# Set-up by halves of the images, in a four-layer convolution kernel on one Trainium2 core

## Chip, cores and metric

The kernel runs on one core of a Trainium2 chip. Its time is the device time of one execution in microseconds (us). Five engines with instruction queues of their own take part: TensorE (PE, with its weight loads PEld), VectorE (DVE), ScalarE (ACT), GpSimd (POOL) and SyncE (SP), which here only issues DMAs.

## Reference

Four layers, each adding a function of the group-normalised input to the input. The change lies wholly in the start of layer 0, whose function is a matrix in tensor-train form with three cores.

```python
def _gn(v, G=8, eps=1e-5):
    B_, H_, W_, C_ = v.shape
    g = v.reshape(B_, H_, W_, G, C_ // G)
    m = jnp.mean(g, axis=(1, 2, 4), keepdims=True)
    s = jnp.var(g, axis=(1, 2, 4), keepdims=True)
    return ((g - m) / jnp.sqrt(s + eps)).reshape(v.shape)
...
# x: (1024, 16, 16, 16) float32
x = x + _L0_conv_ref(_gn(x), L0_conv_core0, L0_conv_core1, L0_conv_core2)
x = x + _L1_conv_ref(_gn(x), ...)
x = x + _L2_conv_ref(_gn(x), L2_conv_filters, L2_conv_bias)
x = x + _L3_conv_ref(_gn(x), ...)
```

The normalisation of layer 0 needs, for every image and each of 8 groups of 2 channels, the mean and the variance over the whole image: no value of an image can be normalised before the whole image has been read.

## The kernel before

**Layer 0.** The 1024 images are two blocks of 512 (the constant NB). The layer's 4096x4096 matrix is cut into blocks, and the block products are taken by a table of fast-multiplication terms (OUTER, 13 entries, and inside each INNER, 7 entries). One entry of OUTER is a *phase*; it has four *units* (q = 0 to 3); a unit has seven *products*, named in INNER: s2, s5, w11, s1, s7, w01, w00. Each product is done in two *halves* (`go(0)` and `go(1)` in `pieces`, L1565), so a phase is 56 halves. A half is four matmul calls of 128x128 weights on 128x256 data (L1586); a call leaves two records in the profile, so a half is eight records.

**What a unit needs.** `build(u, h)` (L1466) makes the weights w00, w01 (h = 0) or w10, w11 (h = 1) of unit u: 16 small matmuls of `gq`, which comes from the tensor-train cores, with `R` into four PSUM banks (L1478), then four copies by ACT (L1483). `mix` (L1508, L1510) adds or subtracts two such weights on DVE: s2, s5, s1, s7, w01. `gather` (L1616) adds a product from PSUM into the unit's result `r`, on ACT for the first use of a quarter and on DVE later.

**The data of phase 0.** Its images are the first 512. A phase's data has four blocks (b, n): b is the half of the image's columns, n is the half of the images (n = 0 is images 0 to 255, n = 1 is 256 to 511). Of INNER, s2 multiplies block (0,0), w11 block (1,0) (after (0,0) has been taken off it), s5 block (1,1), w00 block (0,1); s1, s7 and w01 multiply the sums E0, E1, E2 that `combined` (L1220) makes of several blocks on DVE.

**The set-up, in order of the program** (L2059 to L2110). SP loads the first 512 images as eight transfers of 1 MB (L1091), all of them at once. `stats` makes one BN_STATS per image group, channel group and half image on DVE, 64 in all (L1103); `aggregate` joins them (L1133); `root`, `newton` and `widen` turn them into mean and 1/deviation (L1136 to L1151); `spread` transposes these (L1159, copied by ACT at L1160). `turn` (L1105) transposes the images: four transposes into one bank, then a copy by ACT; there are 32 turns, 16 of them (`lines[0]`) ahead of the first product and 16 (`lines[1]`) woven into phase 0. Only then `first_normed` subtracts the mean and multiplies (L1191) block by block.

Meanwhile `early` (L663) makes the g of units 0 and 1, and `keep_g` (L649) stores it into DRAM with 12 transfers on POOL; `gload` (L1439) reads it back as `gq`. Twelve later pieces of g (`piece`, L680) are made between the halves of phase 0.

**Order.** Every engine runs its instructions in the order in which the program states them; there is no scheduler. `before` (L2090) is a table: the half of phase 0 with that number is preceded by these steps. `run` (L2006) spreads further lists over the halves of a phase between two fractions; `part_steps(1)` makes the data of phase 1 on DVE, between 0.43 and 0.99 of phase 0.

Of the kernel before, what the change touches and what calls it, by code (L numbers as in the profile page):

```python
# [21 lines left out]
P = 128  # L22
# [83 lines left out]
def conv_preact_kernel(ctx: ExitStack, tc: tile.TileContext, a: dict, out: bass.AP):  # L106
# [484 lines left out]
    def train_setup(room):  # L591
# [71 lines left out]
        def early():  # L663

            g = work([P, 2, 8, P], "w0", "gw")
            pg = [bank([P, 2, 4, 64], "w", "pg") for _ in range(4)]
            for x in range(2):
                for k in range(4):
                    for r in range(4):
                        gmul(pg[r][:, x, k], 0, k % 2, x, r, k // 2)  # L670
            for q, x, r in product(range(2), range(2), range(4)):
                f = 64 * x + 16 * r
                A.copy(
                    g.rearrange("p q (o i) f -> p q i o f", i=2)[:, q, :, :, f : f + S],
                    pg[r][:, x, 2 * q : 2 * q + 2].rearrange("p i (o j) -> p i o j", j=S),
                )
                if (x, r) == (1, 3):
                    keep_g(0, q, g[:, q].rearrange("p (o i) f -> p o (i f)", i=2), G)
# [399 lines left out]
    def input_steps(n, tag, queue):  # L1078
# [4 lines left out]
        slots = flats[1 - n].rearrange("p (s f) -> p s f", s=8)  # L1083
        X = part_lines(0)

        def slot(half, bg):
            return slots[:, 0 if (n, half, bg) == (1, 1, 3) else 4 * half + bg]

        def load(half, bg):
            b0 = n * NB + bg * P  # L1090
            queue.dma_start(  # L1091
                slot(half, bg),
                a["x"][b0 : b0 + P, 8 * half : 8 * half + 8].rearrange("b h w c -> b (h w c)"),
            )
# [10 lines left out]
        def turn(h, wh):  # L1105
            pt = bank([P, 4, P], tag[h % len(tag)], "ptin")
            for bg in range(4):
                x = slot(h // 8, bg).rearrange("p (h w f) -> p h w f", h=8, w=2)
                T.transpose(pt[:, bg], x[:, h % 8, wh], ident)
            pt = pt.rearrange("p g b -> p (g b)")  # L1110
            if n == 0 and h < 8:
                if wh:
                    A.copy(X[:, 1, h], pt)
                else:
                    A.copy(raw[:, h], pt.rearrange("p (n i) -> p n i", n=2))
                return
            if h % 2 == 0:
                st["l"] = work([P, 2, NB], "t4", "lines")
            A.copy(st["l"][:, h % 2], pt)
            if h % 2 == 1:  # L1120
                nc.sync.dma_start(
                    xr[n][wh, h - 1 : h + 1].rearrange("h p b -> p h b"), st["l"]
                )
# [32 lines left out]
        def spread(k):  # L1156
            pt = bank([P, 4, P], tag[0], "ptmr")
            for bg in range(4):
                T.transpose(pt[:, bg], st["e", k][:, bg], ident)  # L1159
            A.copy(mr[n][:, k], pt.rearrange("p g b -> p (g b)"))  # L1160

        def kept(b):
            to = xr[n][b, 0:8]
            if b:
                G.dma_start(to.rearrange("h p b -> p h b"), X[:, 1])
                return
            for i in range(2):
                G.dma_start(
                    to.rearrange("h p (n b) -> p h n b", n=2)[:, :, i], raw[:, :, i]
                )  # L1170
# [15 lines left out]
        return loads, stat, lines, tail, [lambda: spread(0), lambda: spread(1)], kept  # L1186
# [6 lines left out]
    def first_normed(b, i):  # L1193

        X, E = part_tile(0)
        cols = slice(256 * i, 256 * i + 256)

        def op(t, k):
            x = X[:, b, t : t + 4, i]
            centre_scale(x, x if b else raw[:, t : t + 4, i], 0, cols, k)  # L1200

        return [(1.2, lambda t=t, k=k: op(t, k)) for t in (0, 4) for k in range(2)]
# [201 lines left out]
    def layer_train():  # L1404
# [60 lines left out]

        def build(u, h):  # L1466

            if u >= len(units):
                return
            R, gs = st["R", units[u][0]], list(st["g", u, h].values())  # L1470
            w = st["w", u, h] = work([P, 2, 2, 4, P], "w1" if h else "w0", "w")
            pw = [bank([P, 2, 2, P], "w", "pw") for _ in range(4)]
            for v in range(2):
                for i in range(2):
                    for k, g in enumerate(gs):
                        for r in range(4):
                            rows = slice(32 * r, 32 * r + 32)
                            T.matmul(  # L1478
                                pw[r][:, v, i], g[rows, P * (2 * v + i) : P * (2 * v + i) + P], R[rows, k],
                                start=k == 0, stop=k == len(gs) - 1,  # L1480
                            )
            for r in range(4):
                A.copy(  # L1483
                    w.rearrange("p b s t m -> p (b s t) m")[:, :, 32 * r : 32 * r + 32].rearrange(
                        "p k (v o) -> p v k o", v=2
                    ),
                    pw[r].rearrange("p v i (k o) -> p v (i k) o", o=S),
                )
# [4 lines left out]
        def mix(u, what):  # L1493

            if u >= len(units):
                return
            x, y, f, out = dict(
                s2=((1, 0), (1, 1), ALU.add, "s2"),
                s5=((0, 0), (0, 1), ALU.add, "s5"),
                s1=((1, 1), (0, 0), ALU.add, "s2"),  # L1500
                s7=((0, 1), (1, 1), ALU.subtract, "s5"),
                w01=((1, 0), (0, 0), ALU.subtract, None),
            )[what]
            into = block(u, 0, 1)
            x, y = block(u, *x), block(u, *y)
            if out:
                t = st[what, u] = work([P, 2, 4, P], out, what)
                V.tensor_tensor(t.rearrange("p s t m -> p (s t m)"), x, y, f)  # L1508
            else:
                V.tensor_tensor(into, x, y, f)  # L1510
# [7 lines left out]
        begun = set()  # L1518
# [46 lines left out]
        def pieces(u, k):  # L1565

            ph, q = units[u]
            what, where, goes = INNER[k]

            def go(i):  # L1570
                X, E = part_tile(ph)
                if i == 0:
                    at = {1: (1, 6144), 3: (1, 14336)}.get(u)
# [9 lines left out]
                po, at = st["po"], 2 * k + i  # L1583
# [3 lines left out]
                if at == 1 and u > 0:  # L1587
                    store(u - 1)
                if at == 2:
                    mix(u, "s1")  # L1590
                if at == 4:
                    mix(u, "s7")
                if at == 5:
# [5 lines left out]
                if at == 9:  # L1599
# [3 lines left out]
                if at == 12:  # L1603
# [5 lines left out]
                if i == 1:  # L1609
                    gather(u, k, po, goes)  # L1610
# [5 lines left out]
        def gather(u, k, po, goes):  # L1616
            r = st["r", u].rearrange("p s a (n i) -> p s (a n) i", n=2)
            at = {x: 2 * x[0] + x[1] for x in goes}
            if k in (2, 3, 6):
# [4 lines left out]
            for x, sign in goes.items():  # L1624
                out = r[:, :, at[x]]
                if all(x not in INNER[j][2] for j in range(k)):
# [6 lines left out]

        steps = [
            [x for u in range(4 * ph, 4 * ph + 4) for k in range(7) for x in pieces(u, k)]
            for ph in range(NP)
        ]
        return (coefs, gload, build, mix), steps
# [420 lines left out]
    with ExitStack() as es:  # L2059
        stage(es, dict(t4=4, s=2, n=2, w1=1, w0=2, s2=1, s5=1, r=1, gq=2, R=2, A=1), dict(w=4, m=1, o=3))  # L2060
        sums, cores, early, rest, sum_steps = train_setup(flats[0][:, 8192:9216])
        tag = ["w"]
        loads, stat, lines, tail, (spread0, spread1), kept = input_steps(0, tag, nc.sync)
        now(loads)

        A.activation(work([P, NB], "n", "warm")[:, 0:1], ident[:, 0:1], AF.Sqrt)
        (coefs, gload, build, mix), phases = layer_train()
        now([sums])
        coefs(0)
        now([cores] + stat[0])  # L2070
        early()
        gload(0, 1, queue=G)
        gload(0, 0, queue=G)
        now(lines[0])
        kept(0)
        kept(1)
        gload(1, 0)
        gload(1, 1)
        build(0, 1)
        build(0, 0)  # L2080
        now(stat[1] + tail[:2])
        mix(0, "s2")
        now([spread0] + tail[2:] + [spread1])
        x00, x11, x10, x01 = (first_normed(*at) for at in ((0, 0), (1, 1), (1, 0), (0, 1)))
        now(x00[0::2] + x00[1::2])
        mix(0, "s5")
        now(x11[:2])
        tag[0] = "m"
        more = combined(0)
        before = {  # L2090
            1: x11[2:] + rest[0][0:1],
            2: x10 + rest[0][1:2] + more[0:2],
            4: more[2:4],
            5: more[4:6],
            7: x01,
            8: more[6:8],
            9: more[8:10],
        }
        free = (12, 15, 18, 22, 26, 29, 32, 36, 40, 43)
        for i, piece in zip(free, rest[0][2:] + rest[1]):  # L2100
# [13 lines left out]
        for j in late:  # L2114
            sums_late(j)
        run(
            steps_of(phases[0]), 107, (), (lines[1], 0.12, 0.42), (part_steps(1), 0.43, 0.99),
        )
        tag.append("w")
        loads, stat, lines, tail, more, _ = input_steps(1, tag, G)  # L2120
# [4 lines left out]
        for i in range(4):  # L2125
            woven_in += [stat[1][i], stat[2][i]] + lines[1][4 * i : 4 * i + 4]
        run(
            steps_of(phases[1]), 107, (), ([(0, x) for x in loads[:7]] + [8] + woven_in + tail, 0.0, 0.76),
# [92 lines left out]
```

## Time and profile before

| | us |
|---|---|
| three runs of the kernel before | 2737.14 median (2736.14 to 2738.66) |
| the profiled execution | 2737.21 |
| its span in the profile | 2734.2 (so 3.0 lie outside the span) |
| PE busy | 2668.0 (98% of the span) |
| DVE busy | 1994.9 (73%) |
| ACT busy | 1241.6 (45%) |
| POOL busy | 542.9 (20%) |

Busy time by stretch of the first 260 us, from the windows of the trace (PEclk is the granted clock of TensorE, 1.00 at full):

| stretch, us | PE busy | DVE busy | ACT busy | PEclk |
|---|---|---|---|---|
| 0 to 30 | 16.4 | 25.9 | 14.4 | 1.00, 1.00, 0.95 |
| 30 to 40 | 5.64 | 5.79 | 2.70 | 0.50 |
| 40 to 50 | 5.26 | 8.27 | 2.59 | 0.50 |
| 50 to 60 | 10.00 | 9.86 | 2.58 | 0.69 |
| 60 to 70 | 10.00 | 10.00 | 3.73 | 1.00 |
| 70 to 80 | 8.50 | 9.93 | 4.07 | 1.00 |
| 80 to 130 | 49.7 | 23.1 | 18.3 | 1.00 |
| 130 to 180 | 50.0 | 45.9 | 14.6 | 1.00 |
| 180 to 190 | 7.24 | 9.96 | 0.00 | 0.83 |
| 190 to 260 | 69.0 | 56.5 | 28.7 | 1.00 |

A line of the timeline reads: start, time from the first start to the last end, engine, line of the kernel, operation, result and sources, shape, number of records, and in brackets the idle time before it with what ended it. The first half of a product begins at 46.93 us; from there on PE is busy almost without a break to the end of the kernel.

### The profile page before, as it was taken

Reading aid. Unit: us, or ns where it says so; the run is one execution under the profiler, and the core shown is the slowest. Engines: PE = TensorE matmul, PEld = TensorE weight load, DVE = VectorE, ACT = ScalarE, POOL = GpSimd, SP = SyncE. Lnnn points to the kernel's source line nnn. Section 1 sums busy time; section 2 is a strip of 40 time slices with the busy share of each in tenths; the row PEclk is TensorE's granted clock in tenths of the full one; section 3 lists DMA queues with packets and bytes.
Section 4 is the critical chain, followed back from the end, with each engine's and each line's share of the span. In section 5 each row is a group of like instructions: output and inputs, shape, how many; then the busy total and the mean of one; then the engine's idle time right before and its main releaser. Section 6 shows DMA issues by size and latency. Waiting matters only on the chain.

```text
span 2734.2 us, 47225 instructions
## 1 busy us (share of the span) xinstructions
PE 2668.0 (98%) x18990; PEld 1749.5 (64%) x18990; DVE 1994.9 (73%) x2414; ACT 1241.6 (45%) x2091; POOL 542.9 (20%) x702
## 2 busy tenths in 40 slices
PE   6999999999999999999999999999999999999997
PEld 5888888888888888888878733433333333334344
DVE  8597667867788776667888677668779858756654
ACT  3324222222232222323322366676767757676664
POOL 2001351312122632311321111111113211110000
PEclk8999999999999999999999999999999999999998
DMA  6687788998797887888689664455576865444665
GB/s 255 214 317 271 228 173 220 240 202 199 188 250 182 156 216 186 205 237 250 178 188 259 138 170 101 107 161 121 107 195 84 202 155 139 99 89 118 179 176 209
DMA packets 265945, 503.19 MB, mean 184 GB/s; under 512 B 34404, under 2 KB 102040, under 8 KB 256448
## 3 DMA queue, kind: packets, MB, share of 16 engines
q1 hardware_dynamic: 179600, 336.68, 36.9%
q0 software_dynamic: 85936, 163.37, 34.0%
q8 instruction: 150, 2.46, 0.4%
q14 instruction: 67, 0.55, 0.1%
q10 hardware_dynamic: 192, 0.13, 0.0%
HBM read 281.71 MB, written 226.49 MB: 186 GB/s over the span
## 4 chain that ended last, share of the span: by engine, by line
PE 84%; DVE 7%; DMA 5%; issue 2%; ACT 1%; SPq 1%; POOL 0%; DVEq 0%; POOLq 0%; ACTq 0%
PE po L1586 40%; PE ph L1993 21%; PE po L1822 8%; PE po L1677 5%; PE pw L1478 4%; DMA xn<-in_x_dram 1%; DVE xn L1191 1%; PE po L1686 1%; DMA xn<-xr 1%; DMA g_sum<-g_dram 1%; DMA xn<-xf 1%; PE ptx L1886 1%; DVE xn L1220 1%; DMA xb<-xn 0%; PE pcnt L1862 0%
## 5 line engine op out<-in xcount | busy, mean ns | idle before, releaser
L1996 ACT ACTIVATE hid<-ph,pack 128x512 f32<-128x512 f32 (+1 forms) x1040 | 641.4, 684 | 313.5 <-PE ph L1993 254.6
L1586 PE MATMUL po<-xn,s 128*128 128x256 f32 x3328 | 756.0, 384 | 10.1 <-DVE s L1508 7.4
L1586 PEld LDWEIGHTS po<-xn,s 128*128 128x128 f32 x3328 | 628.5, 191 | 113.1 <-issue 16.1
L1586 PE MATMUL po<-xn,w 128*128 128x256 f32 x2496 | 565.2, 382 | 1.5 <-DVE xn L1220 1.5
L1993 PE MATMUL ph<-xn,wq 32*128 32x512 f32 (+1 forms) x3752 | 518.3, 590 | 1.9 <-DVE u L1834 1.5
L1586 PEld LDWEIGHTS po<-xn,w 128*128 128x128 f32 x2496 | 468.1, 190 | 74.6 <-issue 5.9
L1483 ACT COPY w<-pw 128x512 f32<-128x512 f32 x416 | 213.6, 599 | 455.6 <-PE pw L1478 379.9
L1993 PEld LDWEIGHTS ph<-xn,wq 32*128 32x128 f32 x3752 | 233.6, 184 | 228.9 <-issue 210.0
L1993 PE MATMUL ph<-xn,pack 32*128 32x512 f32 x1288 | 274.2, 607 | 5.6 <-DVE u L1834 1.6
L1508 DVE TENSOR_TENSOR s<-w 128x1024 f32<-128x1024 f32 x208 | 251.3, 1218 | 29.0 <-PE po L1586 25.9
L1822 PE MATMUL po<-hid,pack 128*32 128x512 f32 (+1 forms) x2080 | 256.0, 592 | 0.8 <-ACT hid L1996 0.5
L1834 DVE SCALAR_TENSOR_TENSOR u<-po,pack,xn 128x512 f32<-128x512 f32 (+1 forms) x130 | 96.3, 741 | 168.1 <-PE po L1822 167.0
L1876 POOL DMA_DIRECT2D xf<-u x96 | 82.6, 861 | 618.7 <-DVE u L1874 591.0
L771 DVE TENSOR_TENSOR xn<-xn,m 128x1024 f32<-128x1024 f32 x128 | 150.2, 1217 | 34.7 <-ACT m L794 34.6
L1993 PEld LDWEIGHTS ph<-xn,pack 32*128 32x128 f32 x1288 | 115.6, 184 | 90.8 <-issue 63.2
L1822 PEld LDWEIGHTS po<-hid,pack 128*32 128x32 f32 x2080 | 53.9, 109 | 174.9 <-ACT hid L1996 86.3
L1677 PE MATMUL po<-xn,convw 128*128 128x512 f32 x368 | 163.6, 598 | 0.0
L1220 DVE TENSOR_TENSOR xn<-xn 128x1024 f32<-128x1024 f32 x130 | 152.6, 1215 | 0.0
L1478 PE MATMUL pw<-R,gq 32*128 32x128 f32 x3328 | 139.4, 286 | 7.9 <-DVE small L1133 7.3
L1622 DVE TENSOR_TENSOR r<-r,po 128x1024 f32<-128x1024 f32 x78 | 95.0, 1218 | 70.5 <-PE po L1586 57.5
L1478 PEld LDWEIGHTS pw<-R,gq 32*128 32x128 f32 x3328 | 113.9, 188 | 42.2 <-issue 38.6
L1560 POOL DMA_DIRECT2D xf<-xn x69 | 88.6, 1733 | 254.2 <-DVE xn L1553 72.3
(230 smaller groups left out, 2764.7 us busy)
## 6 DMA issues: line engine op xcount, KB each, us to landing
xn<-xf SPq DMA_DIRECT2D x128, 512.0 KB
xn<-xb SPq DMA_DIRECT2D x36, 1024.0 KB
wq<-L_conv_wy SPq DMA_DIRECT2D x192, 192.0 KB
xf<-xn POOLq DMA_DIRECT2D x69, 512.0 KB, 9.7
piece<-xb SPq DMA_DIRECT2D x64, 512.0 KB
xf<-r POOLq DMA_DIRECT2D x48, 512.0 KB, 11.7
xf<-u POOLq DMA_DIRECT2D x96, 256.0 KB, 4.1
gq<-g_dram SPq DMA_DIRECT2D x86, 256.0 KB
```

The source lines that it names most:

```text
L771: V.tensor_tensor(part, part, m().unsqueeze(1).broadcast_to([P, 2, NB]), op)
L1220: V.tensor_tensor(out, y, z, f)
L1478: T.matmul(pw[r][:, v, i], g[rows, P * (2 * v + i) : P * (2 * v + i) + P], R[rows, k], start=k == 0, stop=k == len(gs) - 1,)
L1483: A.copy(w.rearrange("p b s t m -> p (b s t) m")[:, :, 32 * r : 32 * r + 32].rearrange("p k (v o) -> p v k o", v=2), pw[r].rearrange("p v ...
L1508: V.tensor_tensor(t.rearrange("p s t m -> p (s t m)"), x, y, f)
L1586: T.matmul(po[:, i], matrix(u, what)[:, i, t], x, start=t == 0, stop=t == 3)
L1622: V.tensor_tensor(part, part, po.unsqueeze(2).broadcast_to([P, 2, 2, 256]), ALU.add)
L1677: T.matmul(st["po", h][wh], conv["fw"][:, y], X[:, 16 * wh + h + y - 1], start=y == max(0, 1 - h), stop=y == min(2, S - h),)
L1822: T.matmul(po[32 * j : 32 * j + 32], nca["w1"][:, v], hid[j], start=v == 0, stop=v == 1)
L1834: V.scalar_tensor_tensor(u, po, nca["b1"], X[:, 8 * q + w2, cols(hf)], ALU.add, ALU.add)
L1993: T.matmul(ph, w, x, start=k == 0, stop=k == len(tiles) - 1)
L1996: A.activation(h, ph, AF.Relu, bias=nca["bt"][:, r : r + 1])
```

## The change

The set-up is divided by images. The loads of images 0 to 255 come first (both halves of each image). Their statistics, mean and deviation are finished by themselves (`first_images`, with `root`, `newton`, `widen` and `spread` taking the half i), and only the turns that they need stand ahead of the first product: 8 of 32. A turn now takes two lines of 256 images instead of one of 512.

The g of units 0 and 1 goes from the tile `gw` straight to the tiles that `build` reads, with 32 transfers of 32 rows by 256 values (32 KB), 16 on SP and 16 on POOL. Behind them on SP follow the four loads of images 256 to 511, and then the stores of g to DRAM, which POOL had.

The order of the products of units 0 and 1 is s2 of unit 0, s2 of unit 1, w11 of unit 0, w11 of unit 1 (four products that use images 0 to 255 alone), then the other five of unit 0 and of unit 1. The two w11 results stay in PSUM until `catch_up` gathers them. The statistics of the rest stand on DVE among these halves, and 20 turns, the two remaining builds and the second `spread` stand on PE before half 8; the last four turns stand before halves 12 and 14. `part_steps(1)` begins at 0.3 of phase 0. In phase 1 an empty stretch of the plan becomes 11 instead of 8.

```diff
-        def early():
+        def early(to, after):
...
+            for q in range(2):
...
+                for o, t, h in product(range(4), range(2), (1, 0)):
+                    (nc.sync if h else G).dma_start(
+                        to[q, h][32 * o : 32 * o + 32, 256 * t : 256 * t + 256],
+                        gs[q][64 * h + t : 64 * h + 64 : 2, o],
+                    )
+            after()
+            for q in range(2):
+                keep_g(0, q, gs[q], nc.sync)
...
+        def turn(half, i, wh, h):
+            tag.append(tag.pop(0))
+            pt = bank([P, 2, 2, P], tag[0], "ptin")
+            for l, g in product(range(2), range(2)):
+                x = slot(half, 2 * i + g).rearrange("p (h w f) -> p h w f", h=8, w=2)
+                T.transpose(pt[:, l, g], x[:, h + l, wh], ident)
...
+            order, late = ((0, 2, 1, 3, 4, 5, 6), 2) if u < 2 else (range(7), 0)
...
+                if i == 1 and at == 3 and late:
+                    behind.append(lambda: gather(u, po, goes, made))
...
+            if ph == 0:
+                us = [(0, 0), (1, 0), (0, 2), (1, 2)] + [x for x in us if x[0] > 1 or x[1] not in (0, 2)]
...
-        loads, stat, lines, tail, (spread0, spread1), kept = input_steps(0, tag, nc.sync)
-        now(loads)
+        for bg in range(2):
+            load(0, bg)
+            load(1, bg)
...
+        now([cores, sums])
+        stats(0, 0)
         coefs(0)
-        now([cores] + stat[0])
-        early()
-        gload(0, 1, queue=G)
-        gload(0, 0, queue=G)
-        now(lines[0])
-        kept(0)
-        kept(1)
-        gload(1, 0)
-        gload(1, 1)
-        build(0, 1)
-        build(0, 0)
-        now(stat[1] + tail[:2])
-        mix(0, "s2")
...
+        stats(1, 0)
+
+        early(early_g(), lambda: now([lambda bg=bg, h=h: load(h, bg) for bg in (2, 3) for h in range(2)]))
+        stats(0, 1)
+        stats(1, 1)
+        aggregate(0)
+        aggregate(1)
+        now(turns(0, 0, 0))
+        root(0)
+        widen(0, 0)
+        newton(0)
+        widen(1, 0)
+        spread(0, 0)
+        part = turns(0, 0, 1)
+        now(part[:2])
+        spread(1, 0)
+        build(0, 1)
+        now(part[2:])
+        build(1, 1)
...
+        now(x00[0::2] + x00[1::2])
+        mix(0, "s2")
+        now(x10[0::2] + x10[1::2])
+        mix(1, "s2")
+        now(more[0:2])
...
         before = {
-            1: x11[2:] + rest[0][0:1],
-            2: x10 + rest[0][1:2] + more[0:2],
-            4: more[2:4],
-            5: more[4:6],
-            7: x01,
-            8: more[6:8],
-            9: more[8:10],
+            2: [lambda: stats(0, 2), lambda: stats(1, 2), lambda: stats(0, 3), lambda: build(0, 0)],
+            4: [lambda: mix(0, "s5"), lambda: stats(1, 3), lambda: aggregate(2), lambda: aggregate(3)]
+            + late1[:2],
+            5: [lambda: keep(1, 0), lambda: keep(0, 0)],
+            6: late1[2:] + [lambda: keep(1, 1)] + late0[:2],
+            8: late0[2:] + [lambda: build(1, 0), lambda: keep(0, 1)] + half1[0][:4]
+            + [lambda: root(1), lambda: widen(0, 1), lambda: newton(1)]
+            + half1[0][4:] + [lambda: spread(0, 1), lambda: widen(1, 1)]
+            + half1[1][:2] + [lambda: spread(1, 1)]
+            + x11[0::2] + x11[1::2] + half1[1][2:4],
+            9: [catch_up] + more[2:6],
+            10: rest[:1],
+            11: rest[1:2] + x01[0::2] + x01[1::2],
+            12: half1[1][4:6],
+            13: more[6:10],
+            14: rest[2:3] + half1[1][6:],
+            16: rest[3:4],
         }
...
-        run(
-            steps_of(phases[0]), 107, (), (lines[1], 0.12, 0.42), (part_steps(1), 0.43, 0.99),
-        )
+        run(steps_of(phases[0]), 107, (), (part_steps(1), 0.3, 0.99))
...
-            steps_of(phases[1]), 107, (), ([(0, x) for x in loads[:7]] + [8] + woven_in + tail, 0.0, 0.76),
+            steps_of(phases[1]), 107, (), ([(0, x) for x in loads[:7]] + [11] + woven_in + tail, 0.0, 0.76),
```

## Prediction

> **What bounds the kernel now.** I read the page's busy slices first: PE has 9 tenths or more in all slices but the first and the last, so time can come only from what stands ahead of the first product or from holes in PE later. Then the timeline of the first 70 us:
>
> ```profile
> PE   6999999999999999999999999999999999999997
> ...
> 30.64 2.71 DVE L1103 BATCH_NORM_STATS2 bn<-xn 128x6 f32<-128x256 f32 x8
> ...
> 33.47 2.09 PE L1478 MATMUL pw<-R,gq 32*128 32x128 f32 x32 [7.26 <-DVE small L1133]
> ...
> 41.56 0.35 DVE L1141 RECIPROCAL small<-small 128x32 f32<-128x32 f32 x1 [2.70 <-ACT small L1137]
> ...
> 43.39 4.62 DVE L1191 TENSOR_TENSOR xn<-xn 128x1024 f32<-128x1024 f32 x4
> ...
> 46.93 3.78 PE L1586 MATMUL po<-xn,s 128*128 128x256 f32 x8 [2.63 <-DVE xn L1191]
> ...
> 57.30 3.72 PE L1586 MATMUL po<-xn,s 128*128 128x256 f32 x16
> ```
>
> The last of eight image loads lets the last statistics begin at 30.64. The first build waits 7.26 us; DVE is named, but POOL's read of g out of DRAM, issued at 29.44, is the likelier releaser (such reads land 4.8 us after issue). The first half-product starts at 46.93 and takes 3.78 us; from 57.30 two take 3.72. The windows show why: the granted clock is 0.50 from 28.9 to 56.2 us.
>
> The third view is PE at the end of phase 0, with three windows of DVE:
>
> ```profile
> 175.58 7.17 PE L1586 MATMUL po<-xn,w 128*128 128x256 f32 x32
> 185.51 8.83 PE L1586 MATMUL po<-xn,s 128*128 128x256 f32 x32 [2.76 <-DVE s L1508]
> ```
> ```profile
> 90.00:100.00 10.00, 10.00 (x66) 8.71 (x65) 2.45 (x2) 5.21 (x15) 0.00 (x0) 1.00 0.89 285
> 100.00:110.00 10.00, 9.70 (x89) 8.00 (x88) 3.58 (x3) 4.72 (x11) 0.00 (x0) 1.00 0.57 207
> ...
> 170.00:180.00 10.00, 10.00 (x75) 8.54 (x74) 10.00 (x10) 2.05 (x4) 0.00 (x0) 1.00 0.96 318
> ```
>
> PE ends phase 0 at 182.75, waits 2.76 us for DVE, and does four halves in 8.83 instead of 7.17 at a clock of 0.50. DVE (third of the busy columns) is idle three quarters of the time around 95 us and full at 175: its work for phase 1 starts late.
>
> **The change, step by step.** Durations are this trace's: a statistic 0.34 (2.71/8), a DVE operation on 1024 columns 1.14 from one start to the next, a half 1.73 to 1.8 (3.78 at half clock), a build 1.1 on PE (2.1) and 2.05 on ACT, a turn 0.44 on PE (0.86) and 0.50 to 0.59 on ACT.
>
> *Ahead of the first product.* Statistics may start at about 7.7 (an estimate: before, they began unwaited at 8.81, behind `coefs`, now second). 32 at 0.34, `coefs` 0.8 and 16 aggregations at 0.087 end at 20.8; four 1 MB loads at the 410 GB/s of the windows are in by 15. Root, newton and widen, on half the columns, take 2.1 (before 41.27 to 43.47): 22.9. Block (0,0), four operations: 27.5. On PE, g takes 3.7 us from about 10, its 16 ACT copies 2.8, to 16.5; turns and spreads follow, build (0,1) runs at 23.9 to 26.0 on PE and to 28.05 on ACT; s2 is ready at 29.2. Two turns and build (1,1) stand ahead of half 0 and need banks that ACT still reads, to 30.9. First half at **31**, 16 us earlier.
>
> *The moves of g.* No row shows one 32 KB tile-to-tile transfer. The nearest are the small weight loads: L607 on SP, four in 2.22 us, L614 on POOL, four in 2.25 and landed 2.2 later. So eight take 4.5 to issue, and those of build (0,1), from 15.2, are in by 22: under the cover of the statistics. [...] The rows show issues 0.56 apart with several under way, so I take the rows. Bounds: 0 and 3 us.
>
> *SP's queue.* It had nothing between 8.1 and 35.7 us; now it has 16 moves, four loads (issued from 23, in at about 34; DVE wants them from 37), 12 stores of g (0.65 to 0.75 each to issue), and four stores of turned images. The line stores behind them free the buffers of turns: 6 MB at 300 to 400 GB/s need 15 to 20 us from 34, and the last waits for its turn to near 56 anyway, so I count nothing. POOL has 16 moves in place of its stores and reads; at 0.56 each they are in by 27, ahead of build (0,0).
>
> *Halves 0 to 7.* I take the clock as cold for halves 0 and 1: 31 to 38.6. Build (0,0) to 40, halves 2 and 3 to 43.5, two turns, halves 4 and 5 to 47.9, four turns at ACT's pace, halves 6 and 7 to 53.8. DVE alongside: block (1,0), s2 of unit 1, the subtraction to 37.3, 24 statistics, s5, eight more, aggregation to 50.7. It then needs a square root that stands on ACT behind six turns and build (1,0).
>
> *The new wait.* Behind half 7 ACT has two copies, the build's 2.05, eight copies, root and spread: 1.1 + 2.05 + 4.4 + 0.7 = 8.2. So DVE starts on block (1,1) at **62**, after idling some 10 us. Queued behind are all sums, and PE's half 8.
>
> *From 62 to half 18.* DVE, from its start on (1,1): block 4.6, s1 5.7, two gathers of 0.6 to 6.9, E0 to 9.2, E1 to 11.5, gather, s7 to 13.3, w01, block (0,1) to 19.0, gather 20.2, E2 to 22.5. PE follows: half 8 at 3.5, halves 10, 11 at 8.1 and 10.9, 12 at 13.5, 14 at 21.3 (after a hole of 2.3), 18 at 29.4. So half 18 stands at 91.4. Before, it stood at 97.76, and 85.0 us later phase 0 was done. That stretch had five turns (2.4) that are now done, and one piece of g less (1.04): 83.6, to 175.0 instead of 182.75: **7.75 us**.
>
> *The boundary.* From half 18 to phase 1, DVE has some 56 operations of 1.14, seven of 0.6 and `coefs`: 68 us in 83.6, because its part begins at 0.3 instead of 0.43. So the hole of 2.76 goes and with it the cold halves behind it (8.83 - 7.17 = 1.66): **4.4 us**. Next late there is the load of phase 1's data, wanted 5 us after it lands. The 11 in phase 1 moves statistics that PE doesn't wait for (0 to 1 us either way; I take 0).
>
> *The sum.* 7.75 + 4.4 = 12.1 us off the profiled execution's 2737.21 (span 2734.2 and 3.0 outside it), which stands within 0.1 of the median of the runs: **2725**.
>
> [...] Here the clock came back 3.4 us after it fell behind the hole at 185, but only at 56.2 after work that began at 46.93, 9.3 us. PE works nearly without break from 21.7 on in the new order. [...] By the row it is 2725; I take the row, since it is the same place of the kernel. [...]
>
> **Rivals.**
> 1. *The boundary stays.* DVE is full to the end as before, since its steps wait for loads and stores that now queue on SP. For it: two DMA waits of 1.93 and 0.62 us in that stretch before. Against: 15 us of slack. Only 7.75 is won: 2729.5.
> 2. *The lead is hidden.* All products beyond the four need images 256 to 511, which are normalised later than before (62 against 49), so a longer wait there eats the lead. If line buffers, loads or ACT's order cost another 8 us, block (1,1) starts at 70: 2733.
> 3. *Slower: the clock.* PE's work is cut by waits and stays at half clock through halves 0 to 7 and their turns. Then, from 31: eight halves 30.2, build 2.1, six turns 5.2: 68.5; the block behind half 7, now PE's, 11.9: block (1,1) at 80.4, 18.4 late, less 12.1: 6.3 slower, 2743.5. It decides once block (1,1) starts after 74. For it: 27 us at 0.50 before. Against: from half 0 to half 7 PE hardly idles, and continuous work always brought the clock back within 9.3 us.
> 4. *It doesn't do what it says:* half 0 still waits for all loads. The order of instructions excludes that: its waits are on the first four.
>
> **Chances and range.** Forecast 0.45 (2722 to 2728), with the warm clock 0.15 more (2718 to 2722), rival 1 0.14, rival 2 0.15, rival 3 0.10; rest 0.01. Three executions lie within 0.1%; 0.2% (5.5 us) is what can be told from no change, so faster means below 2731.7. That takes the forecast, the warm case, rival 1 and a little of rival 2: 0.77; rival 2's rest and a milder rival 3: 0.13; slower 0.10. The range runs from the warm case with a cheap block (DVE could start it at 53.3 at best) to rival 2: 2716 to 2736.
>
> **What would show it.** First half near 31; DVE idle for about 10 us ahead of a start on block (1,1) near 62, ended by ACT; a hole of some 2 us ahead of half 14 at full clock; half 18 near 91; phase 1 starting near 175 with no hole and a clock of 1.00. A wait of build (0,1) for the moves beyond 24, a clock of 0.50 beyond 40, or a hole at phase 1 would make it wrong.

## The result and the profile after

| | before | changed |
|---|---|---|
| median of the runs, us | 2737.39 (2736.14 to 2738.66, 4 runs) | 2724.81 (2722.89 to 2727.75, 4 runs) |
| ratio to before | | 0.9954, 95% interval 0.9942 to 0.9966 |
| profiled execution, us | 2737.21 | 2722.89 |
| its span, us | 2734.2 | 2720.6 |
| PE busy, us | 2668.0 | 2662.2 |
| DVE busy, us | 1994.9 | 1994.4 |

The changed kernel is faster by 12.6 us in the medians; 12.1 was forecast. The work is nearly the same (DVE's busy time differs by 0.5 us), so the gain is idle and half-clock time of PE. The summary page of the profile has PE's busy slices and its clock:

```profile
PE   7999999999999999999999999999999999999997
...
PEclk9999999999999999999999999999999999999998
```

The first slice is busier than before (7 instead of 6), and nothing else can be seen at this scale: a slice is 68 us. The timeline of PE shows the places that the prediction named: build (0,1) at 24.84, the first half, half 8, half 14 and the first four halves of phase 1.

```profile
22.57 1.91 PE L1123 MATMUL ptin<-ident,xn 128*128 128x128 f32 x8
...
24.84 2.27 PE L1579 MATMUL pw<-R,gq 32*128 32x128 f32 x32
...
31.11 3.72 PE L1693 MATMUL po<-xn,s 128*128 128x256 f32 x16
34.77 1.17 PE L1579 MATMUL pw<-R,gq 32*128 32x128 f32 x32
...
43.87 1.04 PE L1123 MATMUL ptin<-ident,xn 128*128 128x128 f32 x8
...
63.21 3.72 PE L1693 MATMUL po<-xn,s 128*128 128x256 f32 x16 [1.82 <-DVE xn L1280]
...
81.02 5.41 PE L1693 MATMUL po<-xn,w 128*128 128x256 f32 x16 [1.78 <-DVE xn L1309]
...
176.03 7.07 PE L1693 MATMUL po<-xn,s 128*128 128x256 f32 x32
```

The first product begins at 31.11 instead of 46.93, at once at full speed: two halves take 3.72, where before one took 3.78. There is a hole ahead of half 8 and another ahead of half 14; behind the second, two halves take 5.41. Phase 1 starts without a hole, 9.5 us earlier than before. The windows of the same trace give the clock, the third number from the end of each line (the columns are as in the prediction):

```profile
20.00:30.00 10.00, 7.43 (x58) 6.22 (x58) 8.96 (x33) 5.07 (x11) 2.29 (x5) 1.00 0.59 181
30.00:40.00 10.00, 9.92 (x95) 8.45 (x96) 10.00 (x14) 5.45 (x11) 0.00 (x0) 1.00 1.01 385
...
80.00:90.00 10.00, 8.98 (x44) 7.43 (x45) 6.79 (x7) 2.10 (x9) 0.00 (x0) 0.83 0.36 115
```

In these records the clock is 1.00 from 20 to 80 us, where before it was 0.50 from 28.9 to 56.2; it is lost once, at the hole ahead of half 14. Ahead of 26 us the durations say otherwise: the eight transposes at 22.57 take 1.91 us and build (0,1) 2.27, where the same work takes 1.04 and 1.17 later, so PE ran at about half speed there. So it did in the kernel before, whose transposes went through at 12 and 11 in the two windows of 2 us up to 22 us and at 20 and 21 in the next two, with 1.00 in all four: the column PEclk can't be relied on so early. Now DVE, which feeds half 8 and phase 1:

```profile
56.84 0.25 DVE L1158 RECIPROCAL small<-small 128x16 f32<-128x16 f32 x1 [5.38 <-ACT small L1154]
...
59.66 4.63 DVE L1280 TENSOR_TENSOR xn<-xn 128x1024 f32<-128x1024 f32 x4 [1.34 <-ACT xn L1178]
```
```profile
127.61 1.22 DVE L1731 TENSOR_TENSOR r<-r,po 128x1024 f32<-128x1024 f32 x1 [0.87 <-issue]
136.37 1.23 DVE L1280 TENSOR_TENSOR xn<-xn,xn 128x1024 f32<-128x1024 f32 x1 [7.54 <-DMA xn<-xr]
```

The first pair is the new wait: DVE had its statistics at 51, waits 5.38 us for ACT's square root and more for `spread`, and begins block (1,1) at 59.66. The second pair was not foreseen: DVE stands still for 7.54 us for a load of phase 1's data. The moves of g on SP and POOL:

```profile
13.91 5.75 SPq L679 DMA_DIRECT2D gq<-gw  x8
19.76 5.00 SPq L679 DMA_DIRECT2D xn<-gw  x8
24.81 2.24 SPq L1104 DMA_DIRECT2D xn<-in_x_dram  x4
```

The last move on SP is issued by 24.8, and the four loads follow at once. Build (0,1) ran at 24.84 behind PE's own work (its line above has no wait), so it did not wait for the moves.

### The profile page after: what moved, and what is told of

Same layout as the page of the kernel before. It is cut to its first block, busy times and chain, and to the rows that moved or that the text cites. A ratio compares the mean times of both kernels' runs of the same rounds, so it can differ in the third digit from the quotient of the medians.

```text
span 2720.6 us, 47297 instructions
## 1 busy us (share of the span) xinstructions
PE 2662.2 (98%) x18990; PEld 1744.2 (64%) x18990; DVE 1994.4 (73%) x2422; ACT 1241.3 (46%) x2094; POOL 539.2 (20%) x701
## 4 chain that ended last, share of the span: by engine, by line
PE 87%; DVE 7%; DMA 2%; issue 1%; ACT 1%; SPq 1%; POOL 0%; DVEq 0%; ACTq 0%
PE po L1693 43%; PE ph L2105 21%; PE po L1934 8%; PE po L1789 5%; PE pw L1579 4%; PE po L1798 1%; DMA xn<-xf 1%; PE ptx L1998 1%; DVE xn L1280 1%; DVE xn L1309 1%; PE ptin L1215 1%; DVE u L1946 0%; DVE s L1608 0%; DMA xn<-in_L_conv_fc_w_dram 0%; DVE xn L778 0%
## 5 line engine op out<-in xcount | busy, mean ns | idle before, releaser
L778 DVE TENSOR_TENSOR xn<-xn,m 128x1024 f32<-128x1024 f32 x128 | 150.2, 1217 | 34.6 <-ACT m L801 34.5
```

The lines of the kernel that those rows point to most:

```text
L778: V.tensor_tensor(part, part, m().unsqueeze(1).broadcast_to([P, 2, NB]), op)
```

## The experiments

Each kernel is the changed one with one edit, or the kernel before where that is said. The times are medians; beside these runs the kernel before took 2737.4 to 2738.0.

| kernel | us (range, runs) | ratio to before [95%] |
|---|---|---|
| changed, again | 2724.83 (2722.97 to 2727.18, 5) | 0.9955 [0.9942, 0.9967] |
| g through DRAM | 2733.17 (2731.76 to 2736.45, 10) | 0.9984 [0.9975, 0.9994] |
| before, PE kept busy | 2737.98 (2735.86 to 2739.79, 10) | 1.0001 [0.9992, 1.0011] |
| two products ahead | 2730.99 (2726.79 to 2731.43, 7) | 0.9972 [0.9961, 0.9983] |
| two ahead, root first | 2727.70 (2725.68 to 2729.68, 4) | 0.9964 [0.9950, 0.9977] |
| root first | 2723.32 (2721.08 to 2724.93, 4) | 0.9949 [0.9935, 0.9962] |
| turns spread | 2721.81 (2717.91 to 2722.77, 5) | 0.9941 [0.9928, 0.9953] |
| hole filled | 2725.88 (2722.63 to 2727.52, 4) | 0.9957 [0.9944, 0.9971] |
| part_steps late | 2728.44 (2726.12 to 2729.48, 5) | 0.9967 [0.9954, 0.9980] |
| before, part_steps early | 2741.99 (2736.54 to 2749.16, 10) | 1.0020 [1.0011, 1.0030] |
| fourth load early | 2723.72 (2722.97 to 2726.10, 4) | 0.9951 [0.9937, 0.9964] |
| turns spread, fourth load early | 2720.47 (2715.64 to 2721.61, 5) | 0.9930 [0.9916, 0.9944] |

**Is the early start carried by the moves of g?** The 32 transfers are taken out, and g goes through DRAM on POOL as before.

```diff
...
-                for o, t, h in product(range(4), range(2), (1, 0)):
-                    (nc.sync if h else G).dma_start(
...
-            after()
+                keep_g(0, q, gs[q], G)
             for q in range(2):
-                keep_g(0, q, gs[q], nc.sync)
+                for h in (1, 0):
+                    G.dma_start(to[q, h], g_dram[0][0, q, h].rearrange("o s k f -> (o s k) f"))
+            after()
```

> The changed kernel with the g of units 0 and 1 stored to DRAM and read back by POOL as before, and no tile-to-tile moves; the loads of images 256 to 511 then stand on SP without anything ahead of them. Theory (the moves carry the early start): the first build waits for g to about 33, half 0 starts near 41 instead of 31, block (1,1) near 68 instead of 59.7, and 7 to 9 us are lost, 2733. Rival (ACT and DVE hide it, as the statistics of the rest end at 51 anyway): 0 to 2 us, 2726.

The build, in PE's timeline of this kernel, and then s2 on DVE:

```profile
33.46 2.09 PE L1576 MATMUL pw<-R,gq 32*128 32x128 f32 x32 [8.71 <-DMA gq<-g_dram]
```
```profile
37.62 1.23 DVE L1605 TENSOR_TENSOR s<-w 128x1024 f32<-128x1024 f32 x1 [9.51 <-ACT w L1581]
```

The build waits 8.71 us for g and starts at 33.46, as in the kernel before (33.47), although the statistics of half the images are long done. Half 8 goes from 63.21 to 71.80 and phase 1 from 176.03 to 183.98 (in the slowest of this kernel's ten executions, 2736.45), and the time rises by 8.4 us. So two thirds of the gain hang on the moves: all the rest of the change together (statistics by halves, the order of the products, the early `part_steps`) is worth 4.2 us without them. The statistics by halves were not run by themselves.

**What did the cold clock cost before?** In the kernel before, 60 transposes (`busy`) into a bank that nothing reads keep PE busy ahead of the first half.

```diff
...
         now(lines[0])
+        busy(24)
...
-        now([spread0] + tail[2:] + [spread1])
+        now([spread0])
+        busy(16)
+        now(tail[2:] + [spread1])
+        busy(20)
```

> The kernel before with 60 transposes whose result nobody reads, on PE where it idles before the first product, so that the clock is full at half 0. Rival theory (the cold clock cost the kernel before its 5 us): halves 0 and 1 in 1.8 instead of 3.8 us each and 5 us faster, 2732. My theory (behind them DVE sets the pace to 77 us): warm halves wait for block (1,0) and E2 instead, at most 1 us, 2737.

```profile
47.08 1.99 PE L1586 MATMUL po<-xn,s 128*128 128x256 f32 x8 [0.82 <-DVE xn L1191]
...
60.16 6.75 PE L1586 MATMUL po<-xn,w 128*128 128x256 f32 x16 [3.44 <-DVE xn L1220]
```

The first half now runs in 1.99 instead of 3.78, and the clock is 1.00 from 44 to 58 us (0.50 from 40 to 42), so here the transposes brought it back in time. The time doesn't move: PE reaches half 4 earlier, waits there 3.44 us for DVE's sums, and starts it at 60.16 instead of 60.85. So up to half 4 DVE set the pace in the kernel before, and the cold clock cost 0.7 us at most. More this run can't say, since behind the new wait two halves ran cold (6.75 instead of 3.62).

**Are four products ahead worth their trouble?** Here w11 is taken early in unit 0 only, and unit 1 keeps its old order; two products, not four, stand ahead of block (1,1). The steps of halves 4 to 8 stand joined ahead of half 4, and the later ones are numbered down by four.

```diff
...
-            order, late = ((0, 2, 1, 3, 4, 5, 6), 2) if u < 2 else (range(7), 0)
+            order, late = ((0, 2, 1, 3, 4, 5, 6), 2) if u < 1 else (range(7), 0)
...
-                us = [(0, 0), (1, 0), (0, 2), (1, 2)] + [x for x in us if x[0] > 1 or x[1] not in (0, 2)]
+                us = [(0, 0), (0, 2)] + [x for x in us if x[0] > 0 or x[1] not in (0, 2)]
...
```

> The changed kernel with only s2 and w11 of unit 0 ahead; unit 1 runs in its old order. Theory (the start of block (1,1) sets the next 30 us): with two products fewer in front, ACT reaches the mean and the deviation sooner, block (1,1) starts near 54, and of the 7.2 us of the two products put back all but some 1 us is regained, 2726. Rival (a product ahead is worth its own time): 7 us lost, 2732.

The timeline of ACT shows a wait that the expectation hadn't counted:

```profile
54.47 0.39 ACT L1178 COPY xn<-ptmr 128x256 f32<-128x256 f32 x1
61.18 1.07 ACT L1130 COPY lines<-ptin 128x512 f32<-128x512 f32 x2 [6.32 <-DMA xr<-lines]
```

With less work ahead, ACT comes to the turns sooner than the stores that free their line buffers, and it waits 6.32 us with the second `spread` queued behind. DVE can subtract the mean in block (1,1) at 55.29 but multiply by 1/deviation only at 62.57. So 6.2 us are lost to two things together, the two products and this wait. The next kernel takes them apart: two products ahead, and the square root and both spreads put ahead of build (1,0) and the turns (as in the experiment after it).

> e7_two_ahead with mean and deviation of images 256 to 511 ahead of build (1,0) and of the turns, as in e3_root_first. In e7 the deviation came to 62 because ACT waited 6.3 us for a line buffer whose store stood behind 4 MB of other stores. Theory (that wait alone took the 5 us): block (1,1) is whole by 60, and the two products put back cost 1 us, 2726. Rival (a product ahead is worth its own time; the gathers still wait for ACT's copies behind the same line buffers): 1 us sooner than e7 at most, 2730.

It took 2727.70: the wait for stores is gone from ahead of the spreads, and block (1,1) starts at 53.46. Against the same order with four products ahead, the next experiment (2723.32), it is 4.4 us slower, and phase 1 starts at 179.15 against 175.07. That is what the two additional products ahead bring in this order.

**Does the block of work behind half 7 matter?** Step 8 puts the square root and the spreads ahead of the turns and of the last build.

```diff
-            8: late0[2:] + [lambda: build(1, 0), lambda: keep(0, 1)] + half1[0][:4]
-            + [lambda: root(1), lambda: widen(0, 1), lambda: newton(1)]
-            + half1[0][4:] + [lambda: spread(0, 1), lambda: widen(1, 1)]
-            + half1[1][:2] + [lambda: spread(1, 1)]
+            8: late0[2:] + [lambda: root(1), lambda: widen(0, 1), lambda: newton(1), lambda: widen(1, 1)]
+            + [lambda: keep(0, 1), lambda: spread(0, 1), lambda: build(1, 0), lambda: spread(1, 1)]
+            + half1[0] + half1[1][:2]
```

> The changed kernel with root, widen, newton and both spreads of images 256 to 511 ahead of build (1,0) and of ten turns, instead of behind and between them. Theory (the order of ACT is what DVE waits 6.7 us for): block (1,1) starts near 54 instead of 59.7; but the two gathers behind it need copies that ACT makes only after its last turn at 62, so E0 comes some 2 us sooner, half 14 too, 2722.5. Rival (DVE is idle there at no cost, PE's turns decide): half 8 and half 14 stay, 2725.

```profile
54.31 4.63 DVE L1280 TENSOR_TENSOR xn<-xn 128x1024 f32<-128x1024 f32 x4 [1.79 <-DMA xr<-xn]
58.86 1.22 DVE L1608 TENSOR_TENSOR s<-w 128x1024 f32<-128x1024 f32 x1
63.46 0.69 DVE L1741 TENSOR_TENSOR r<-r,po 128x512 f32<-128x512 f32 x1 [3.38 <-ACT r L1737]
```

Block (1,1) starts 5.35 us earlier and now waits for a store of turned images instead of ACT (1.79 us), but the time falls by only 1.5 us, less than the intervals tell apart. The turns still stand ahead of half 8 on PE and ahead of ACT's first gathers, so half 8 moves by only 1.15 us (62.06), and DVE waits 3.38 us for ACT one step later. Both have to move: in the next kernel, besides, only 6 of step 8's 14 turns stay there, and the other eight stand two by two ahead of later halves; the last four turns and the fourth late piece of g stand ahead of half 14. (Step 8 is the one above with `half1[0][:4]` in place of its third line, ahead of the two `x11`.)

```diff
-            10: rest[:1],
-            11: rest[1:2] + x01[0::2] + x01[1::2],
-            12: half1[1][4:6],
-            13: more[6:10],
-            14: rest[2:3] + half1[1][6:],
-            16: rest[3:4],
+            10: rest[:1] + half1[0][4:6],
+            11: rest[1:2] + half1[0][6:] + x01[0::2] + x01[1::2],
+            12: half1[1][:2],
+            13: more[6:10] + half1[1][2:4],
+            14: half1[1][4:] + rest[2:4],
```

> The changed kernel with the order of e3_root_first, only six turns (two, then four) ahead of half 8, the other ten put ahead of halves 10 to 14, and the fourth piece of g ahead of half 14. Theory: block (1,1) starts near 54, half 8 near 57, half 14 near 75 instead of 81 without a hole and at full clock, half 18 near 83 instead of 92: 8 to 9 us faster than the changed kernel, 2716. Rival (line buffers and DVE take it back): 2 to 4 us, 2722.

```profile
59.34 3.62 PE L1693 MATMUL po<-xn,s 128*128 128x256 f32 x16
...
76.90 1.09 PE L1123 MATMUL ptin<-ident,xn 128*128 128x128 f32 x8 [0.28 <-ACT lines L1130]
...
80.00 7.17 PE L1693 MATMUL po<-xn,w 128*128 128x256 f32 x32
```

Half 8 follows at 59.34, 3.9 us earlier than in the changed kernel, and from there to half 14 and beyond PE has one hole, of 0.28. Half 14 gains only 1.0 (80.00 for 81.02), since the eight turns (3.6 us of PE from start to start) and the piece of g (1.04) now stand between half 8 and it; what is won is the hole that they fill and the half clock behind it. Half 18 is at 88.14 (92.08), phase 1 at 172.32 (176.03). The medians differ by 3.0 us.

**Can the hole ahead of half 14 be filled?** The fourth late piece of g (1.04 us of PE) moves from half 16 to half 14.

```diff
-            14: rest[2:3] + half1[1][6:],
-            16: rest[3:4],
+            14: rest[2:4] + half1[1][6:],
```

> The changed kernel with the fourth piece of g ahead of half 14 instead of half 16. Theory: the hole of 1.78 us before half 14 shrinks to 0.75, the clock does not fall, halves 14 and 15 take 3.6 instead of 5.4 us, half 18 comes 2.7 us sooner, 2722. [...]

```profile
63.64 6.46 PE L1693 MATMUL po<-xn,s 128*128 128x256 f32 x16 [0.76 <-DVE xn L1280]
...
82.76 7.07 PE L1693 MATMUL po<-xn,w 128*128 128x256 f32 x32
```

There is no hole at half 14 any more and four halves run there at full speed, but in this execution the clock fell ahead of half 8, where nothing was edited. The time doesn't change: the two kernels differ by 1.1 us, within their ranges.

**What does the early `part_steps` bring?** First it goes back to 0.43 in the changed kernel.

```diff
-        run(steps_of(phases[0]), 107, (), (part_steps(1), 0.3, 0.99))
+        run(steps_of(phases[0]), 107, (), (part_steps(1), 0.43, 0.99))
```

> The changed kernel with the data of phase 1 begun at 0.43 of phase 0, as before, instead of 0.3. Theory (the boundary term of the prediction): DVE is late again, PE waits 2 to 3 us between phases 0 and 1 and does the next four halves at half clock (8.8 instead of 7.1 us), so about 4.4 us of the gain are lost, 2729. Rival (the lead gives DVE the room anyway): no hole, 2725.

```profile
164.84 7.17 PE L1693 MATMUL po<-xn,w 128*128 128x256 f32 x32
174.80 8.83 PE L1693 MATMUL po<-xn,s 128*128 128x256 f32 x32 [2.78 <-DVE s L1608]
```

The hole of 2.78 and the cold halves behind it are back, as they were before the change, and the time rises by 3.6 us. Then the start at 0.3 is put into the kernel before, by itself; the turns woven in have to end earlier for it.

```diff
-            steps_of(phases[0]), 107, (), (lines[1], 0.12, 0.42), (part_steps(1), 0.43, 0.99),
+            steps_of(phases[0]), 107, (), (lines[1], 0.08, 0.29), (part_steps(1), 0.3, 0.99),
```

> The kernel before with the data of phase 1 begun at 0.3 of phase 0, and its 16 woven turns between 0.08 and 0.29 to make room. Theory: the hole of 2.76 us and the cold halves go in the old set-up too, 4.4 us faster, 2733. Rival (the loads of that data wait for turns and stores, and denser turns hold PE): 0 to 2 us, 2736.

```profile
59.57 2.00 PE L1586 MATMUL po<-xn,w 128*128 128x256 f32 x8 [1.20 <-DVE xn L1220]
...
67.49 0.66 PE L1109 MATMUL ptin<-ident,xn 128*128 128x128 f32 x4 [2.07 <-ACT lines L1119]
...
188.68 7.07 PE L1586 MATMUL po<-xn,s 128*128 128x256 f32 x32
```

The hole ahead of phase 1 is gone, and the kernel is slower by 4.5 us: the denser turns, which wait for ACT's copies, hold PE up between halves 4 and 18 (half 18 at 104.18 against 97.76). My theory of it failed. (This execution took 2738.51 us, the second quickest of ten; where the slower ones lose more wasn't profiled.) So in the old set-up, with its turns placed like this, the early start can't be had; the set-up by halves has taken most of the turns out of its way. Other placings of the turns were not tried.

In both kernels with the start at 0.3, PE waits about 0.7 to 1.3 us ahead of halves 38 and 42, and the late start has no such waits. They come from the time in which DVE stands still (7.54 us in the changed kernel). The plan puts the fourth load of phase 1's data later than the other three; the next kernel issues it with them.

```diff
-        steps = loads[: 3 if j == 1 else 4] + [8]
+        steps = loads + [8]
...
-            if p == 1 and j == 1:
-                steps.append(loads[3])
```

> The changed kernel with the fourth load of phase 1's data issued with the other three; it was kept back because of a result that no longer lies in its place. Theory: DVE's wait of 7.5 us for it near 129 goes, and with it PE's two waits of 0.73 before halves 38 and 42: 1.5 us faster, 2723.5. Rival (other DMAs come later for it): 0.

```profile
127.86 1.22 DVE L1729 TENSOR_TENSOR r<-r,po 128x1024 f32<-128x1024 f32 x1 [0.87 <-issue]
129.00 1.22 DVE L1280 TENSOR_TENSOR xn<-xn,xn 128x1024 f32<-128x1024 f32 x1
```

DVE's wait is gone (compare the pair of the changed kernel above, 7.54 us), and so are PE's at halves 38 and 42. From half 18 to phase 1 the trace has 82.16 us, against 83.95 in the changed kernel and 84.10 in its second profile: 1.8 to 1.9 us less. In the medians it is 1.1 us, which can't be told from nothing, as the ranges overlap.

**The two that helped, together.** Turns spread and fourth load early in one kernel, and beside it the changed kernel once more.

> e8_turns_spread and e10_fourth_load together. Theory: phase 0 ends at 170.6, 1.7 us sooner than in e8, 2720. Rival: as e8, 2722.

> The changed kernel as it is, on the same chip, to compare e11 with. 2725. [...]

The combination took 2720.47 us, 4.4 less than the changed kernel on the same chip (2724.83); their ranges don't overlap. Phase 1 starts at 170.88, 5.7 us before the changed kernel's second profile (176.56). Its four halves from half 14 on, and half 8 of the changed kernel's second profile:

```profile
78.90 8.85 PE L1691 MATMUL po<-xn,w 128*128 128x256 f32 x32
```
```profile
64.37 6.66 PE L1693 MATMUL po<-xn,s 128*128 128x256 f32 x16 [0.93 <-DVE xn L1280]
```

Even this version is cold for a part of its way (8.85 instead of 7.17 for four halves), and the unedited program lost its clock this time ahead of half 8 (6.66 instead of 3.72 for two halves) and not of half 14.

## Why the prediction came true, step by step

**First half near 31: right** (31.11), with its parts within 1.6 us: statistics begin at 9.26, after a wait of 1.76 for the first load (7.7 was estimated), are joined by 21.7 (20.8), block (0,0) starts at 23.66 (22.9).

**The moves: right in the main.** Issues are 0.68 us apart on SP and 0.51 on POOL (0.56 was taken). The eight that build (0,1) reads were issued by 19.7, under the statistics; the last on SP came later, by 24.8, and build (1,1), which reads them, did not wait for them either. POOL's sixteen took 3.2 and 1.8 us from issue to landing (medians of eight each), but one was issued every 0.51 us, so that several lay side by side, and build (0,1) started at 24.84. Taking the moves away cost 8.4 us.

**"I take the clock as cold for halves 0 and 1": wrong.** Halves 0 and 1 took 3.72, not 7.6, and half 7 ended at 49.53, not 53.8. PE was at half speed when it took up work at 22.09, and at full speed some 4.5 us later, by the durations above; it has no hole of more than 0.5 us from there to half 0. I had let the cold time begin with half 0. Even the row's 9.3 us, counted from 21.7, where I had PE's work begin, end at 31.0. The time to full clock was not the same in every run. In the ten profiles of kernels with this start PE works from about 22 us on without a longer hole, yet in one (`part_steps` late) the clock came back during build (0,1) at 24.60 (1.80 us, for 2.27 in the changed kernel; 0.83 in the window from 20 to 30, so 3.4 us at half clock), and in another (turns spread and fourth load early, 0.54 and 0.77 in the two windows of 10 us from 20) it was full again only at 34.6, 12.9 us after PE took up work at 21.68. Seven have 3.72 for the two halves, three have 4.94, 5.03 and 6.09; none has the 7.6 of my sum. No run shows the term behind the range given to the warm clock (2718 to 2722): the changed kernel had halves 0 and 1 warm and half 7 done 4.3 us ahead of my sum, and took 2724.81.

**"ACT block of 8.2": right in kind, mis-sized.** From the end of half 7 to block (1,1) it was 10.1 us. I had added ACT's copies only; but ACT and PE alternate: ACT's first pair of copies waited 0.6 us for its transposes, two later pairs 0.26 each, and the build's copies 1.08 for its matmuls. So block (1,1) started at 59.66 instead of 62, since the two errors, 4.3 early and 1.9 late, have opposite signs. That this wait bounds the gain only in part is shown by the kernels with the root first: moving it alone gave 1.5 us, which can't be told from nothing, moving the turns with it 3.0.

**From block (1,1) to half 18: 29.4 was 32.4.** Half 8 at +3.55 and half 14 at +21.36 are as forecast (3.5 and 21.3), the hole 1.78 for 2.3. Behind it came 1.7 us of half clock (5.41 for 3.72), which is not in the prediction's sum, and a piece of g (1.04) that I had counted behind half 18. Half 18 stood at 92.08 (91.4).

**Half 18 to phase 1: right in the number, not in its parts** (83.95 for 83.6). The piece of g that I added here (1.04) stands ahead of half 18, as just said, and PE's two waits of 0.73 took its place in the sum. They come from a thing unforeseen, DVE's wait of 7.54 for the fourth load, worth 1.8 to 1.9 us in the traces: with that load early the stretch is 82.16. I had named "the load of phase 1's data" as next late and put it in phase 1's own start, not here.

**The boundary: right.** The hole and the cold halves are gone (4.4 was forecast for them). By the late start the trace loses 2.78 and 1.76 there, 4.5, and wins back 1.6 between half 18 and the end of phase 0 (82.3 for 83.95), where the waits at halves 38 and 42 are missing. So the early start is worth 2.9 us there; in the medians the late one is 3.6 slower.

**The sum.** At the end of phase 1's first four halves the profile stands 11.2 us ahead (194.34 to 183.1), where 12.1 was forecast. The spans differ by 13.6. Most of the last 2.4 us arises at one place late in layer 0, where PE of both kernels waits equally long for DVE:

```profile
1356.98 8.70 PE L1586 MATMUL po<-xn,s 128*128 128x256 f32 x32 [2.37 <-DVE s L1508]
```
```profile
1345.43 7.15 PE L1693 MATMUL po<-xn,s 128*128 128x256 f32 x32 [2.37 <-DVE s L1608]
```

Up to there the lead is 11.6 us, 0.3 more than at the start of phase 1, so the 11 in that phase, put at nothing, was worth no more than this. Behind that hole four halves ran cold in the kernel before and at full speed in the changed one, and the lead is 13.1. I put it down to chance and not to the change: in its second profile the same changed kernel has a mean clock of 0.995 instead of 0.997 and a span of 2724.3, 3.7 longer, with phase 1 only 0.5 us later. So that the forecast came within 0.5 us of the medians' 12.6 is partly luck: the cold halves (4.3 too much), the block of ACT (1.9 too little) and the way from there to half 18 (3.0 too little) nearly cancel, and two executions of one program differ by more than what is left.

Of the rivals, "the boundary stays" is excluded by the trace. "The lead is hidden" needed block (1,1) at 70; it came at 59.66. "Slower: the clock" needed half clock to half 7; none was there. Its premise, that waits would keep PE cold, did not hold: PE was busy for 9.92 of the ten us from 30 and 9.76 of the ten from 40. But what I held against it, that continuous work brings the clock back within 9.3 us, is too strong as well, with the 12.9 above. And the experiment in the kernel before shows that there the cold halves cost 0.7 us at most up to half 4, because DVE was later.

## What to carry to other kernels

Where a reduction over all data stands ahead of the first product, make it by parts and order the products so that those of the first part come first, but look for the other input of the first product: here the weights' way through DRAM took two thirds of the gain away when it was put back. Behind such a lead, count the engines that alternate as one chain (the transposes of PE and the copies of ACT), and put what a third engine waits for (here a root of 0.2 us and two copies) ahead of the bulk work. A plan that starts earlier wants its loads earlier, too: here one load that was left in its place made DVE wait 7.54 us.

## What the runs showed of the hardware that was not expected

Holes of the same length do not do the same to the clock. Ahead of half 8 the changed kernel idled 1.82 us and stayed at full speed (3.72 for two halves); the kernel with the fourth load early, whose program is the same up to there, idled 1.83 and fell to half (5.40 for two). The same steps stand ahead of half 8 in six profiles, and in five of them the clock fell there: behind holes of 1.52, 1.83 and 1.83 us, and behind 0.76 and 0.93 with one of 2.3 shortly before. In the changed kernel's two profiles the clock fell once ahead of half 14 and once ahead of half 8, and with the root first a hole of 1.16 us ahead of half 14 was enough (5.41).

What the records do show is the length of the stretches at half clock. In the changed kernel's profile it is 3.41 us (81.12 to 84.53). The kernel before has 27.3 us (28.9 to 56.2), eight times that, then 129.7 us at full clock, thirty-eight times that, and again 3.41 at half (185.94 to 189.35). In the changed kernel's second profile it is 6.8 us, twice that (0.68 in the window from 60 to 70, 0.98 from 70 to 80). Why the clock fell behind one hole and not behind another of the same length is not shown by any run. For a sum of this kernel it means that a hole of some one to two us is priced at its length and, by chance, at some half clock behind it, 1.7 to 3 us as measured (5.41 and 6.66 for 3.72).

In the fastest version the clock fell at about 79 us (windows of 2 us: 0.73 from 78, 0.50 from 80) though PE's longest hole in the 20 us before was 0.28; the kernel with the turns spread has the same order there and kept its clock. Why is open.

Thirty-two transfers of 32 KB from tile to tile, issued 0.5 to 0.7 us apart on two queues, took 11 us to issue in all, and nothing that reads them waited: the 1.8 to 3.2 us that POOL's took to land lay side by side.
